# A four-layer convolution and attention sequence: the last layer's 3x3 convolution by minimal filtering, its experts mixed a stage earlier

## The chip, the cores and the metric

The kernel runs on one core of a Trainium2 chip. The metric is the device time of one execution in microseconds (us); lower is better. The core has TensorE (PE, its weight loads PEld), VectorE (DVE), ScalarE (ACT), GpSimd (POOL) and SyncE (SP, which here only issues DMAs). Each engine works through its own queue in order.

## What is computed

The input is 8 images of 512 channels, 32 x 32 pixels, fp32. Four layers follow each other. Layer 0: group norm, q, k, v, attention with 8 heads, three steps of an inner iteration, a projection. Layer 1: attention over one head with q and k of 64 channels. Layer 2: separable up- and downsampling with a leaky ReLU between. Layer 3 is the one that the change is about: a bottleneck whose weights are mixed for each image out of 8 experts.

```
pooled = x.mean(axis=(2, 3))
rw = jax.nn.sigmoid(pooled @ router_w.T + router_b)       # 8 weights per image
W = jnp.einsum('be,eoihw->boihw', rw, experts)            # for w1, w2, w3
out = relu(bn1(conv1x1(x, W1)))                           # 512 -> 128 channels
out = relu(bn2(conv3x3(out, W2)))                         # 128 -> 128
out = relu(bn3(conv1x1(out, W3)) + x)                     # 128 -> 512
```

## The kernel before, in words

`tile_sequence` handles one image after another through layers 0 to 2 (`layer0`, `layer1`, `layer2`), and puts each image's result z (2 MB) to DRAM (`spilled`). Layer 3 then runs over all 8 images. The last image's z stays in SBUF. Activations lie with channels on the partitions: `[128, 4, 1024]`, 16 KB a partition, out of one pool of seven buffers (`big_tile`). PSUM is split into `ps_sc` (two pairs of banks), `ps_tp` and `ps_mm` (two banks each).

A scheduler orders the instructions of each engine, by the order of the program among what it thinks ready, so that a later stage's work may move ahead on an engine that it takes for idle. Inside `tc.manual_schedule(engines=...)` the named engines keep the order in which the code is written: that is so for PE, DVE and ACT in layer 0's attention, and for PE in `layer2`.

What matters for the change:

- `layer0` makes q, k and v by `product`: seven products P1, C11, U2, U3, C22, C21, C12 of quarter matrices, each some TensorE work followed by a `made` step that takes PSUM away. For q and k (`channels`) ACT copies P1 before C11 goes on in the same bank and takes C11; DVE takes the rest. For v (`positions` with a row) DVE takes all. The code writes three such products after each other; an `Exp` of one element ("early") behind k loads ACT's table ahead of attention.
- Attention runs 64 steps; per step ACT takes an exponential of 128 x 1024 into one of six `tmp` buffers, and DVE adds it into a `sums` buffer (two exist), two SBUF inputs.
- The inner iteration is three `product`s with tanh on ACT and sums on DVE.
- `layer2_constants` (L133) builds the up- and downsampling operators from iotas and filter taps: 14 iotas and two broadcast loads on POOL, many small DVE instructions. It stands in image 0's layer 1, behind the value product.
- `out_of_bounds` (L1218) counts overflows and loads the verdict into a register of every engine, for a second pass that is normally skipped. In the code it stands ahead of layer 3; the register loads of PE, DVE and ACT were scheduled at the very end.
- Layer 3 before: all experts are held in SBUF, w1 in a pool of its own and three thirds of w2 and w3 in four big buffers, loaded during layer 2 of the last image. `route` makes the weights of images 0 to 6 at once, and of image 7 later. `mixed(b)` (L1204) makes an image's weights: per part one ACT multiplication and seven DVE multiply-adds. It is called one image ahead.
- One image of layer 3: c1 (L324, 2 halves of 4 matmuls of 512 columns), ReLU into a zero-rimmed plane `rim`; c2 (L1272, 9 taps for 2 halves, so 18 matmuls); ReLU into h2; c3 (L1286, 4 blocks of 2), each followed by a DVE multiply-add onto z, an ACT ReLU and an output DMA.

Each fp32 matmul of the program is two TensorE instructions in the profile.

Of the kernel before, what the change touches and what calls it, by code (L numbers as in the profile page):

```python
# [37 lines left out]
QR = C // 2  # L38
PARTS = ("A11", "A12", "-A22", "S1", "S2", "S3", "S4")
# [14 lines left out]
def tile_sequence(ctx: ExitStack, tc: tile.TileContext, a: dict, out: bass.AP, shifted: bool):  # L54
# [78 lines left out]
    def layer2_constants():  # L133

        setup, apart = tmp("setup", S), tmp("setup_apart", S)
# [7 lines left out]
        def iota(name, pattern, base, per_partition=0):  # L143
            t = scratch(name, pattern[0][1])
            nc.gpsimd.iota(
                t, pattern, base=base, channel_multiplier=per_partition,
                allow_small_or_imprecise_dtypes=True,
            )
            return t
# [15 lines left out]
        taps_up = scratch("taps_up", NTAP)  # L165
        nc.gpsimd.dma_start(taps_up, a["up_filter"].partition_broadcast(P))
        nc.vector.tensor_scalar_mul(taps_up, taps_up, 2.0)
        taps_dn = scratch("taps_dn", NTAP)
        nc.gpsimd.dma_start(taps_dn, a["down_filter"].partition_broadcast(P))

        part = iota("part", [[1, 1]], 0, 1)
        tap = iota("tap", [[1, NTAP]], 0)

        def rows_of(name, width):

            row = scratch(f"row_{name}", 1)
            first = iota(f"first_{name}", [[width, (P - 1) // width]], width)
            nc.vector.tensor_scalar(first, first, part, None, ALU.is_le)
            nc.vector.tensor_reduce(row, first, AX.X, ALU.add)
            col = scratch(f"col_{name}", 1)  # L180
            nc.vector.scalar_tensor_tensor(col, row, float(-width), part, ALU.mult, ALU.add)
            return row, col

        def tap_index(name, n, step, base, mul, by):

            t = iota(f"ix_{name}", [[step, n]], base)
            add = scratch(f"add_{name}", 1)
            nc.vector.tensor_scalar_mul(add, by, float(mul))
            nc.vector.tensor_scalar_add(t, t, add)
            return t  # L190

        def outer(op, rows, cols):
# [13 lines left out]


        in_c, in_r = rows_of("in", IR)
        ur = placed("ur", tap_index("ur", UR, -1, 17, -2, in_r), taps_up)
        outer(up_op, ur, placed("uc", tap_index("uc", UC, 1, 11, -2, in_c), taps_up))  # L210
        outer(
            up_left_op, ur, placed("ucl", tap_index("ucl", UC, 1, 11 - 2 * EDGE, -2, in_c), taps_up)
        )
        up_rr, up_cc = rows_of("up", UC)
        outer(
            dn_op,
            placed("dr", tap_index("dr", OR, 2, -6, 1, up_rr), taps_dn),
            placed("dc", tap_index("dc", OC, 2, 0, -1, up_cc), taps_dn),
        )
        in_c, in_r = rows_of("in63", 3)  # L220
        outer(
            up63_op[:, 0 : 2 * W],
            placed("ur63", tap_index("ur63", 1, 0, 10, -2, in_r), taps_up),
            placed("uc63", tap_index("uc63", 2 * W, 1, 5, -2, in_c), taps_up),
        )
        outer(
            dn63_op,
            placed("dr63", iota("dr63", [[2, 3]], 1), taps_dn),
            placed("dc63", tap_index("dc63", W, 2, 6, -1, part), taps_dn),
        )  # L230
# [18 lines left out]
    pooled = const.tile([P, CC, B], F32, name="pooled")  # L249
    spilled = [spill.tile([C, S], F32, name=f"spill_{run}_{b}", tag=f"spill_{b}") for b in range(B)]  # L250
# [338 lines left out]
    def layer0(b, x, norm, w):  # L589
# [8 lines left out]
        q = big_tile(f"q_{b}", [P, CC, S])  # L598
        k = big_tile(f"k_{b}", [P, CC, S])
        v = big_tile(f"v_{b}", [P, SC, C])  # L600
        all_of(product(f"q_{b}", w["q"], h, t, channels(f"q_{b}", q, qkv_b[:, 0:CC])))
        if b == 0:
            nc.vector.tensor_add(row_bias, row_bias, bias2)
        w["inl"] = weight("inl", b)
        all_of(product(f"k_{b}", w["k"], h, t, channels(f"k_{b}", k, qkv_b[:, CC : 2 * CC])))
        w["proj"] = weight("proj", b)
        early = small.tile([P, 1], F32, tag="early", bufs=1, name=f"early_{b}")
        tc.keep_in_program_order(nc.scalar.activation(early, eps, AF.Exp))
        all_of(product(f"v_{b}", w["v"], h, t, positions(f"v_{b}", v, v_row), rows=True))
        w["v1"] = weight("v1", b)  # L610
# [145 lines left out]

        all_of(inner)
        for it in (1, 2):
            t = quarter_sums(f"hf_{b}_{it}", hf)
            name = f"inl_{b}_{it}"  # L760
            all_of(product(name, w["inl"], hf, t, inner_step(name, hf)))
# [7 lines left out]
    def layer1(b, x, w, midway):  # L769
# [77 lines left out]
        if b == 0:  # L847
            layer2_constants()
# [249 lines left out]
    with tc.tile_pool(name=f"weights_{run}", bufs=1) as wpool:  # L1098
# [10 lines left out]
        late_loads()  # L1109

# [20 lines left out]
    WCOLS = 2 * C + 9 * P  # L1131
    experts = {}

    def load_experts(key, n, pool=None):
        if pool is None:
            t = big_tile(f"{key}e", [P, NE, n])
        else:
            t = pool.tile([P, NE, n], F32, name=f"{key}e", bufs=1)
        nc.sync.dma_start(t, a[key])
        experts[key] = t  # L1140
# [6 lines left out]

    load_experts("w1", C, pool3)

# [11 lines left out]
    router_w = pool3.tile([P, CC, NE], F32, name="router_w", bufs=1)  # L1161
    nc.gpsimd.dma_start(router_w, a["router_wT"].rearrange("(cc p) e -> p cc e", p=P))
    router_b = pool3.tile([P, NE], F32, name="router_b", bufs=1)
    nc.gpsimd.dma_start(router_b, a["router_b"].partition_broadcast(P))
    rw = const.tile([P, B, NE], F32, name="rw")

    def route(b0, b1):

        n = b1 - b0
        mean = pool3.tile([P, CC, n], F32, name=f"mean_{b0}", bufs=1)  # L1170
        nc.vector.tensor_scalar_mul(mean, pooled[:, :, b0:b1], 1.0 / S)
        ps = bank(ps_tp, f"router_{b0}")
        for cc in range(CC):
            nc.tensor.matmul(
                ps[0:n, 0:NE], mean[:, cc, :], router_w[:, cc, :],
                start=(cc == 0), stop=(cc == CC - 1),
            )

        apart = pool3.tile([n, n, NE], F32, name=f"apart_{b0}", bufs=1)
        nc.vector.tensor_tensor(  # L1180
            apart, ident[0:n, 0:n].unsqueeze(2).to_broadcast([n, n, NE]),
            ps[0:n, 0:NE].unsqueeze(1).to_broadcast([n, n, NE]), ALU.mult,
        )
        ps = bank(ps_tp, f"routed_{b0}")
        nc.tensor.matmul(
            ps[:, 0 : n * NE], ones[0:n, :], apart.rearrange("k b e -> k (b e)"),
            start=True, stop=True,
        )
        nc.vector.tensor_tensor(
            rw[:, b0:b1, :], ps[:, 0 : n * NE].rearrange("p (b e) -> p b e", e=NE),  # L1190
            router_b.unsqueeze(1).to_broadcast([P, n, NE]), ALU.add,
        )
        nc.scalar.activation(rw[:, b0:b1, :], rw[:, b0:b1, :], AF.Sigmoid)

    route(0, B - 1)


    rims = []
    for i in range(2):
        t = pool3.tile([P, H + 2, W + 2], F32, tag=f"rim_{i}", bufs=1, name=f"rim_{i}")  # L1200
        nc.gpsimd.memset(t, 0.0)
        rims.append(t)

    def mixed(b):  # L1204
        wt = pool3.tile([P, WCOLS], F32, tag="mixed", name=f"mixed_{b}")
        parts = [("w1", 0, C)]
        parts += [(f"w2_{ky}", C + ky * 3 * P, 3 * P) for ky in range(3)]
        parts += [("w3", C + 9 * P, C)]
        for key, at, n in parts:
            src, dst = experts[key], wt[:, at : at + n]  # L1210
            nc.scalar.activation(dst, src[:, 0, :], AF.Copy, scale=rw[:, b, 0:1])
            for e in range(1, NE):
                nc.vector.scalar_tensor_tensor(
                    dst, src[:, e, :], rw[:, b, e : e + 1], dst, ALU.mult, ALU.add
                )
        return wt

    def out_of_bounds():  # L1218
# [10 lines left out]
        nc.vector.tensor_add(count, count, count0)  # L1229
        ps = bank(ps_tp, "within")  # L1230
# [5 lines left out]
    z3 = {}  # L1236

    def freed(t):
        if t == 4:
            load_experts("w2_0", 3 * P)  # L1240
            z3[0] = load_z(0)
        elif t == 6:
            for ky in (1, 2):
                load_experts(f"w2_{ky}", 3 * P)
        elif t == 7:
            load_experts("w3", C)

    z_last = layer2(B - 1, halo, freed)
    z_next = z3[0]
    redo = None if shifted else out_of_bounds()  # L1250
    wt_next = mixed(0)
    route(B - 1, B)
    for b in range(B):
        z, wt = z_next, wt_next
        if b + 1 < B:
            z_next = load_z(b + 1) if b + 2 < B else z_last
            wt_next = mixed(b + 1)
        h1 = rims[b % 2]
        for g in range(2):
            ps = bank(name=f"c1_{b}_{g}")  # L1260
# [105 lines left out]
```

## Time and profile before

| | |
|---|---|
| time, median of 3 runs | 3780.77 us (3780.32 to 3782.17) |
| the profiled execution's own time | 3779.3 us |
| its span | 3777.5 us, mean granted TensorE clock 0.997 |
| instructions | 50171 |
| DMA | 248.67 MB, mean 66 GB/s over the span |

The page lists busy time by engine, the chain of work that ended last, and groups of instructions. A group's line has source line, engine, operation, output<-inputs, shapes, count, then busy us and mean ns of one, then the idle time before and what released it. A stage table has, per stretch of the span: its length, then busy us and instructions of PE, PEld, DVE, ACT and POOL, the granted clock, the share of the DMA engines and GB/s. A wait line reads: waiting engine, tile and line, what it waited for, then total us, times and longest.

The shape of the run: the start takes 14.7 us, an image 436 to 450 us up to the end of layer 2, and layer 3 the last 247.9 us.

### The profile page before, as it was taken

The numbers are of one execution on the slowest core, as the hardware profiler recorded it, in microseconds if no ns is written. First come the engines' busy times: TensorE is split into PE (matmuls) and PEld (weight loads), VectorE is DVE, ScalarE is ACT, GpSimd is POOL, SyncE is SP. The second block draws the span as 40 slices with busy tenths as digits, with TensorE's granted clock in tenths as the row PEclk, the third lists the DMA queues.
The fourth block names the chain that finished last, engine by engine and source line by source line (L and its number), as shares of the span: only waits on it lengthen the run. The fifth ranks groups of instructions, "written<-read, shape, count | busy, mean of one in ns | idle before, by whom it ended". The sixth has DMA issues, their size and how long they took to land.

```text
span 3777.5 us, 50171 instructions
## 1 busy us (share of the span) xinstructions
PE 3733.1 (99%) x20838; PEld 1985.0 (53%) x20838; DVE 2550.6 (68%) x3589; ACT 1200.6 (32%) x1716; POOL 85.2 (2%) x115
## 2 busy tenths in 40 slices
PE   8999999999999999999999999999999999998998
PEld 4346653475435753476534754367534754357543
DVE  4877548665676648765586657766487656866885
ACT  1631225212442216312352125422262133421332
POOL 4000000000000000000000000000000000001000
PEclk9999999999999999999999999999999999999999
DMA  5002310122101320013101220023201131004432
GB/s 205 21 3 85 120 59 1 52 79 96 40 1 64 120 81 1 17 70 120 59 1 62 96 88 21 1 81 105 80 1 42 65 119 40 1 1 132 157 152 94
DMA packets 86193, 248.67 MB, mean 66 GB/s; under 512 B 10480, under 2 KB 33024, under 8 KB 79168
## 3 DMA queue, kind: packets, MB, share of 16 engines
q1 hardware_dynamic: 70528, 221.67, 16.6%
q10 hardware_dynamic: 13824, 12.59, 1.0%
q0 software_dynamic: 1600, 11.07, 0.8%
q8 instruction: 166, 2.72, 0.3%
q14 instruction: 75, 0.61, 0.1%
HBM read 185.40 MB, written 59.90 MB: 65 GB/s over the span
## 4 chain that ended last, share of the span: by engine, by line
PE 96%; DVE 2%; DMA 1%; issue 0%; ACT 0%; POOL 0%; SPq 0%; ACTq 0%; DVEq 0%; POOLq 0%
PE scores L640 12%; PE av L681 12%; PE inl_X L435 7%; PE up L1019 5%; PE dn L1037 5%; PE inl_A L435 4%; PE v_X L435 4%; PE inl_Y L435 4%; PE av_X L953 4%; PE c L1272 3%; PE v_A L435 3%; PE v_Y L435 3%; PE av_Y L953 3%; PE av_A L953 3%; PE proj_X L435 2%; PE q_X L435 2%
## 5 line engine op out<-in xcount | busy, mean ns | idle before, releaser
L659 ACT ACTIVATE e<-scores 128x1024 f32<-128x1024 f32 x504 | 516.2, 1024 | 668.3 <-PE scores L640 661.4
L640 PE MATMUL scores<-q,k 64*64 64x512 f32 x4096 | 532.1, 592 | 0.0
L681 PE MATMUL av<-e,v 64*64 64x512 f32 x4096 | 528.8, 589 | 0.0
L665 DVE TENSOR_TENSOR acc<-acc,e 128x1024 f32<-128x1024 f32 x320 | 389.3, 1216 | 37.4 <-ACT e L659 35.4
L640 PEld LDWEIGHTS scores<-q,k 64*64 64x64 f32 x4096 | 150.7, 133 | 295.2 <-issue 216.8
L681 PEld LDWEIGHTS av<-e,v 64*64 64x64 f32 x4096 | 156.8, 133 | 282.7 <-issue 276.7
L435 PE MATMUL inl_X<-T_hf,w_inl 128*128 128x512 f32 x576 | 261.6, 592 | 0.0
L1003 DVE SCALAR_TENSOR_TENSOR up<-up,leak 128x512 f32<-128x512 f32 x264 | 173.8, 687 | 125.9 <-ACT leak L1002 120.9
L702 DVE RECIPROCAL inv<-av 128x256 f32<-128x256 f32 x128 | 223.0, 1747 | 2.0 <-PE av L694 2.0
L1002 ACT ACTIVATE leak<-up 128x512 f32<-128x512 f32 x264 | 149.8, 596 | 206.1 <-DVE up L1003 132.9
L1037 PEld LDWEIGHTS dn<-dn_op,up 128*64 128x64 f32 (+1 forms) x4096 | 187.9, 136 | 18.2 <-issue 18.2
L1037 PE MATMUL dn<-dn_op,up 128*64 128x99 f32 (+5 forms) x4096 | 194.0, 253 | 0.0
L1019 PE MATMUL up<-halo,up_op 126*128 126x512 f32 (+1 forms) x384 | 182.0, 601 | 9.4 <-DVE up L1003 9.4
L435 PEld LDWEIGHTS inl_X<-T_hf,w_inl 128*128 128x128 f32 x576 | 108.8, 190 | 138.4 <-issue 112.2
L435 PE MATMUL inl_A<-hf,w_inl 128*128 128x512 f32 x384 | 174.3, 597 | 0.0
L531 ACT ACTIVATE inl_U<-inl_U,inl_b 128x512 f32<-128x512 f32 x96 | 66.7, 718 | 302.7 <-DVE inl_U L546 302.7
L663 DVE TENSOR_TENSOR acc<-e,e 128x1024 f32<-128x1024 f32 x64 | 79.4, 1240 | 107.2 <-ACT e L659 92.4
L542 DVE TENSOR_TENSOR inl_U<-inl_X,inl_P 128x512 f32<-128x512 f32 x96 | 61.8, 685 | 113.9 <-PE inl_X L435 112.9
L1272 PE MATMUL c<-rim,mixed 128*128 128x512 f32 x288 | 125.5, 593 | 0.0
L1019 PEld LDWEIGHTS up<-halo,up_op 126*128 126x128 f32 (+1 forms) x384 | 72.0, 191 | 97.3 <-issue 66.3
L435 PEld LDWEIGHTS inl_A<-hf,w_inl 128*128 128x128 f32 x384 | 71.6, 190 | 97.2 <-issue 86.5
L953 PE MATMUL av_A<-v,eT 128*128 128x256 f32 x512 | 122.3, 384 | 0.0
(299 smaller groups left out, 5534.5 us busy)
## 6 DMA issues: line engine op xcount, KB each, us to landing
halo<-ypad_u SPq DMA_DIRECT2D x128, 252.0 KB
halo<-ypad_u SPq DMA_DIRECT2D x128, 198.0 KB
w_v<-stored_u_v SPq DMA_DIRECT2D x14, 1792.0 KB
x<-in_x_dram SPq DMA_DIRECT2D x32, 512.0 KB
spill_u<-z SPq DMA_DIRECT2D x28, 512.0 KB
z<-spill_u SPq DMA_DIRECT2D x28, 512.0 KB
out_dram<-z SPq DMA_DIRECT2D x28, 512.0 KB
w_q<-stored_u_q SPq DMA_DIRECT2D x7, 1792.0 KB
```

What stands on the lines that cost most here:

```text
L435: nc.tensor.matmul(dst, lhs, rhs, start=(opens and s == 0 and cc == 0), stop=(cc == 1 and s == rows), skip_group_check=True,)
L640: nc.tensor.matmul(ps[r][rows[c]], k[rows[r], oc, jc * P + c * HD : jc * P + c * HD + HD], q[rows[r], oc, ts(sh, HALF)], start=True, stop= ...
L659: nc.scalar.activation(e, pair, AF.Exp, scale=HD ** -0.5)
L665: nc.vector.tensor_add(accs[g], accs[g], e)
L681: nc.tensor.matmul(avs[g][r][rows[c]], v[rows[r], jc, ts(2 * oc + c, HD)], e[rows[r], ts(c, HALF)], start=(jc == 0), stop=(jc == SC - 1),)
L702: nc.vector.reciprocal(copies[g][:, at], totals[g][:, at])
L953: nc.tensor.matmul(ps[:, ts(s, QR)], left[:, j, at : at + P], right[:, j, :], start=(what in ("P1", "U2", "W") and s == 0 and j == 0), sto ...
L1002: nc.scalar.mul(t, ps, 0.2 * SQRT2)
L1003: nc.vector.scalar_tensor_tensor(dst, ps, SQRT2, t, ALU.mult, ALU.max)
L1019: nc.tensor.matmul(ps[i], op[0 : IR * n, :], halo.tile(t)[0 : IR * n, c + i, :], start=True, stop=True,)
L1037: nc.tensor.matmul(rows[part, r0 - first : r1 + 1 - first, c0 : c1 + 1], up[t][0:k, c, ts(2 * cc + s, HD)], op[:, r0 - 4 * t + 3 : r1 + 4 ...
L1272: nc.tensor.matmul(banks[g].rearrange("p (h w) -> p h w", w=W), wt[:, at : at + P], h1[:, ky + 16 * g : ky + 16 * g + 16, kx : kx + W], st ...
```

## The change

Four things change together.

The 3x3 convolution goes by minimal filtering along rows. Two neighbouring outputs of a row need four inputs d0..d3 and three taps g0, g1, g2. `spread` makes d1+d2, d3−d1, d2−d1, d0−d2 on DVE, `transform_weights` makes (g0+g2)/2 ± g1/2 on ACT and DVE, and `c2` multiplies four parts of three rows: 12 matmuls of 512 columns. Two parts are then combined through ACT copies and two DVE instructions. h2 comes out by even and odd columns, and c3 and its evictions follow that (`apart`, a stride of two elements in z).

The experts of image b are mixed in `layer0` of image b+1, by ACT multiplications and POOL additions (`premix`), and the mixed weights go to DRAM (`mixed`). They are read from DRAM for every image, in nine pieces of 256 columns. Layer 3 loads an image's mixed weights from there (`load_weights`). Image 7's experts are mixed inside layer 3, during images 0 to 5. `route` takes one image and broadcasts the mean over 128 columns.

In layer 3, PE, DVE and ACT keep the written order, as do ACT and SP in q, k, v of images 1 to 7. The bounds count moves behind images 5 and 6.

The operators of layer 2 are built in image 0's inner iteration, two sections per step.

```diff
-        all_of(product(f"q_{b}", w["q"], h, t, channels(f"q_{b}", q, qkv_b[:, 0:CC])))
...
+        fixed = tc.manual_schedule(engines={mybir.EngineType.Activation, mybir.EngineType.SP}) if b else nullcontext()
+        with fixed:
+            q = big_tile(f"q_{b}", [P, CC, S])
+            parts = product(f"q_{b}", w["q"], h, t, channels(f"q_{b}", q, qkv_b[:, 0:CC]))
+            for _ in range(2):
+                next(parts)
+            mixing = iter(())
+            if b:
+                mixing = premix(b - 1)
+                next(mixing)
+                route(b - 1, pooled_mean(b - 1))
+            for _ in range(2):
+                next(mixing, None)
+            all_of(parts)
...
+            w["inl"] = weight("inl", b)
+            k = big_tile(f"k_{b}", [P, CC, S])
...
+            for _ in range(2):
+                next(parts)
...
+            tc.keep_in_program_order(nc.scalar.activation(early, eps, AF.Exp))
+            for _ in range(3):
+                next(mixing, None)
+            all_of(parts)
+            w["proj"] = weight("proj", b)
+            for _ in range(2):
+                next(mixing, None)
+            v = big_tile(f"v_{b}", [P, SC, C])
...
+            next(parts)
+            all_of(mixing)
+            all_of(parts)
```

```diff
+    def premix(b, halves=False):
+        half, slots = NE // 2, 2 if halves else 3
+        read = big_tile(f"experts_{b}", [P, 2, NE, QR])
...
+        for i in range(slots):
+            load(i)
+        yield
+        for i, (at, n) in enumerate(pieces):
...
+            scaled(0)
+            scaled(1)
+            if halves:
+                yield
+            added(lo[:, 0:2, :], lo[:, 0:2, :], hi[:, 0:2, :])
+            scaled(2)
+            added(lo[:, 2, :], lo[:, 2, :], hi[:, 2, :])
+            added(lo[:, 0, :], lo[:, 0, :], lo[:, 2, :])
+            scaled(3)
+            added(lo[:, 3, :], lo[:, 3, :], hi[:, 3, :])
+            added(lo[:, 1, :], lo[:, 1, :], lo[:, 3, :])
+            added(dst, lo[:, 0, :], lo[:, 1, :])
+            if i % 2 == 1 or i == len(pieces) - 1:
...
+                nc.gpsimd.dma_start(mixed[b][:, first : at + n], acc[:, 0 : at + n - first])
+            if i + slots < len(pieces):
+                load(i + slots)
+            yield
```

Here `load` is an SP DMA of a piece (the third slot lies in the two `sums` buffers), `scaled(e)` two ACT multiplications, of experts e and e+4, and `added` a POOL addition.

```diff
+    with tc.manual_schedule(engines={engines.PE, engines.DVE, engines.Activation}):
         for g in range(2):
-            ps = bank(name=f"c1_{b}_{g}")
...
+            c1(0, g)
+        mean = pooled_mean(B - 1)
+        transform_weights(0)
+        mixing = premix(B - 1, halves=True)
+        next(mixing)
+        route(B - 1, mean)
+        spreads[0] = spread(0)
+        for b in range(B):
+            more = b + 1 < B
+            if more:
+                if b + 2 < B:
+                    zs[b + 1] = load_z(b + 1)
+                wts[b + 1] = load_weights(b + 1)
...
+            c2(b, main, 1, True, False)
+            nc.scalar.copy(one, main)
+            for _ in range(2):
+                next(mixing, None)
+            c2(b, odd, 3, True, True)
+            c2(b, main, 2, False, False)
+            nc.scalar.copy(two, main)
+            nc.vector.scalar_tensor_tensor(one, one, 2.0, two, ALU.mult, ALU.subtract)
+            nc.vector.tensor_add(one, odd, one)
             nc.scalar.activation(
...
+                h2[:, ts(1, HALF)], one, AF.Relu, bias=bn[1][1], scale=bn[1][0]
+            )
+            if more:
+                for g in range(2):
+                    c1(b + 1, g)
+                transform_weights(b + 1)
+            c2(b, main, 0, False, True)
             nc.scalar.activation(
...
+                h2[:, ts(0, HALF)], main, AF.Relu, bias=bn[1][1], scale=bn[1][0]
+            )
+            if more:
+                spreads[b + 1] = spread(b + 1)
+            next(mixing, None)
+            c3(b, h2)
...
+            if b == 5:
+                count = out_of_bounds()
+            elif b == 6:
+                redo = counted(count)
```

```diff
+    def transform_weights(b):
...
+        nc.scalar.mul(g1, g1, 0.5)
+        nc.vector.tensor_add(even, g0, g2)
+        nc.vector.scalar_tensor_tensor(even, even, 0.5, g1, ALU.mult, ALU.subtract)
+        nc.vector.scalar_tensor_tensor(g1, g1, 2.0, even, ALU.mult, ALU.add)
...
+    def spread(b):
+        d = [rim[:, :, k : k + W - 1 : 2] for k in range(4)]
...
+        nc.vector.tensor_add(to[1], d[1], d[2])
+        nc.vector.tensor_sub(to[3], d[3], d[1])
+        nc.vector.tensor_sub(to[2], d[2], d[1])
+        nc.vector.tensor_sub(to[0], d[0], d[2])
+        return t
...
+        for i in (1, 0):
+            for oc in range(2):
+                multiply(oc, i)
+                if i == 0:
+                    finish(oc)
+        for oc in (2, 3):
+            for i in (1, 0):
+                multiply(oc, i)
+            finish(oc)
```

The last block is the end of the new `c3`; `multiply` is one matmul, `finish` a block's DVE multiply-add, ACT ReLU and output DMA. `c1` and `c3` are the bodies of before as functions, with c1 in `ps_tp` banks.

```diff
+        operators = layer2_constants() if b == 0 else iter(())
+        next(operators, None)
         all_of(inner)
         for it in (1, 2):
...
-            all_of(product(name, w["inl"], hf, t, inner_step(name, hf)))
+            parts = product(name, w["inl"], hf, t, inner_step(name, hf))
+            for i, _ in enumerate(parts):
+                for _ in range(2 if i < 4 else 0):
+                    next(operators, None)
+        all_of(operators)
...
-        if b == 0:
-            layer2_constants()
```

## The prediction

> **What bounds the kernel now.** I read the page's busy times first, then the chain that ended last.
>
> ```profile
> PE 3733.1 (99%) x20838; PEld 1985.0 (53%) x20838; DVE 2550.6 (68%) x3589; ACT 1200.6 (32%) x1716; POOL 85.2 (2%) x115
> PE 96%; DVE 2%; DMA 1%; issue 0%; ACT 0%; POOL 0%; SPq 0%; ACTq 0%; DVEq 0%; POOLq 0%
> ```
>
> TensorE is both the busiest engine and the path. Time is won by giving it fewer instructions or closing its gaps (44 us); POOL is free, ACT two thirds free. Next, busy time by stage: start, image 0, image 1, image 7 up to layer 3, layer 3.
>
> ```profile
> 0.00:14.72 14.72, 1.18 (x5) 1.00 (x5) 9.14 (x30) 2.06 (x3) 5.09 (x14) 1.00 0.89 289
> 14.72:461.90 447.18, 439.73 (x2534) 236.80 (x2534) 309.75 (x468) 138.44 (x198) 45.60 (x57) 0.99 0.22 77
> 461.90:898.00 436.10, 435.85 (x2537) 234.97 (x2535) 289.95 (x398) 139.13 (x200) 3.56 (x4) 1.00 0.17 58
> ...
> 3079.50:3529.60 450.10, 439.78 (x2543) 235.25 (x2541) 298.90 (x420) 145.18 (x211) 13.14 (x20) 0.99 0.18 61
> 3529.60:3777.50 247.90, 237.31 (x558) 102.44 (x556) 193.21 (x292) 80.23 (x104) 0.00 (x0) 0.98 0.32 124
> ```
>
> An image takes 436 us with PE full; image 0 takes 11 us more, image 7 14 us more. TensorE's own waits name why:
>
> ```profile
> PE up L1019 <- DVE up L1003: 9.4, 9, 7.0
> PE xT L857 <- DVE y L858: 5.2, 1, 5.2
> ```
>
> The 5.2 us is image 0's: 58 small operator-building instructions stand on DVE from 328.8 to 354, between the evictions that PE needs. The 7.0 us is image 7's: DVE mixes experts (L1213) from 3470.8 to 3476.4 while PE waits for its leaky ReLU. Last, the TensorE timeline of one layer 3 image (start, length):
>
> ```profile
> 3590.17 7.03 PE L324 MATMUL c<-z,mixed 128*128 128x512 f32 x16
> 3597.03 15.62 PE L1272 MATMUL c<-rim,mixed 128*128 128x512 f32 x36
> 3612.49 7.31 PE L1286 MATMUL c<-h,mixed 128*128 128x512 f32 x16
> 3619.63 7.03 PE L324 MATMUL c<-z,mixed 128*128 128x512 f32 x16
> ```
>
> The 3x3 takes (3612.49 − 3597.03)/36 = 0.4294 us an instruction, two instructions to a matmul. L1286 takes 7.14 instead of 16 × 0.4294 = 6.87: its first weights wait for ACT.
>
> [...] While POOL adds at 92–98 us, DVE's sums (1.22 us otherwise) take
>
> ```profile
> L665 DVE TENSOR_TENSOR acc<-acc,e 128x1024 f32<-128x1024 f32 x3 | 5.4, 1814 | 0.3
> L367 POOL TENSOR_TENSOR w_v<-w_v,raw_v 128x512 f32<-128x512 f32 x1 | 2.3, 2262 | 0.0
> ```
>
> and POOL's add 2.26 for 1.26, whereas DVE's PSUM evictions kept 0.69 beside POOL. [...] After the 7.0 us gap four matmuls took 3.78 us, elsewhere 1.88. [...]
>
> **The change part by part** (against the span of 3777.5 us; the run that was profiled took 3779.3, 1.8 more, and the median of the runs is 1.5 above that).
>
> 1. *Convolution.* Per image 12 matmuls instead of 18: 8 × 12 instructions × 0.4294 = **−41.2**. All on the path. c3 now begins with the half that is ready long before, and 1.7 us of PE work covers the ReLU (0.78) of the other: 8 × 0.27 = **−2.2**.
>
> 2. *The work that the convolution gains.* In order on PE: c2's parts 1, 3, 2 (2.6 us each), c1 of the next image (6.9), part 0, c3; 24.05 us an image. Between c1's end (14.6) and the next image's part 1 (24.05) stand ACT's ReLU 0.77 and halving ~0.6 (384 elements, L1211's 0.60), two DVE steps of 0.61 and four sums of 544 elements (0.72 from 512 in 0.68): done at about 20.1. DVE then begins c3's eviction (1.28), whose first operand is ready at 19.8; c3's last block needs a bank from it at 22.3 and has it at 21.4. DVE per image: 1.4 + 1.8 + 2.9 + 5.4 = 11.5; ACT 9.5 plus 5 of mixing. Both lie under 24. POOL's mixing for image 7 meets the four sums and three other DVE instructions with two SBUF inputs, but POOL is busy some 7 us of an image, mostly before them. *No cost*; the cover is c2's part 0 and c3's first half. The sums' stride of two elements is in no row of this trace: bounded by 0.72 and twice that. At twice, with the evictions' stride too, c3 waits about 3 us an image (24 in all). I take the lower[...].
>
> 3. *Layer 3's start.* PE's c1 for image 0 ends at +6.9; behind it, all in fixed order, stand ReLU, halving, two DVE steps, DVE's router add, the first sum: c2 starts at about +11 less the router's matmuls: **+3.3** (0.8 if the transform is early, 5 with a cooled clock). Image 7 has no c1 between part 2 and part 0, so ACT's copy (0.58 and two semaphores) shows: **+0.9**.
>
> 4. *The register load for the bounds count* now stands in fixed PE order behind image 6's c3. It waits for a bank from DVE's evictions, for DVE's two last evictions (2.7 us) and loads (0.59 in the trace of before, where it lay at the end): **+2.9** (0 to 4).
>
> 5. *Weights from DRAM.* The next image's 1.1 MB go out when c3 of the image before frees the buffer, behind outputs and perhaps a 2.1 MB z load on one SP queue. Needed 7.7 us later. With 1 MB ahead at about 300 GB/s (the window 461–469 moved 262, the start 289 to 382), 2 us to start (1.8 MB stores landed in 6.0 to 7.7 us, some 6 of it transfer) and 0.9 for c1's part, they land at about 6.4. Lead 1.3 us, so I allow **+4** over seven images (0 to 25). Layer 3's transfers, some 46 MB in 200 us, need 230 GB/s.
>
> 6. *Image 7 before layer 3.* The mixing there vanishes from DVE, with it the 7.0 us gap, the 2 us of slow clock behind it and smaller waits: stage 450.1 to about 438: **−11.3**, old routers apart.
>
> 7. *Routing.* Eight routers of eight instructions with a 128-column weight load each. The row of that shape, L832, takes 0.85 us per eight: 6.8, less the old 1.5: **+5.3**.
>
> 8. *Mixing in q, k, v, seven times.* Nine pieces. ACT: 8 × 0.41 (interval of L1211 less a slope of 0.10 per 128) = 3.3 us, 29 in all; POOL 1.24 + 5 × 0.71 = 4.8 us, 41 in all; DMA 8.9 MB. Counting from q's start in image 1 (461.9): z's spill holds the queues to about 469 (262 GB/s in 461–469, nothing after); pieces 0 and 1, 1 MB each at some 300 GB/s, land at 473 and 476, ACT is through at 480, k's first copy is due at 488. SP's inl, proj and later x loads queue behind piece loads that wait for POOL; none is due before attention. Pieces 2 to 8 begin after k's second part (495.5, sigmoid and exp tables 1.28 each included); POOL sets the pace, since piece i+3 is loaded when POOL has added piece i: POOL starts piece 2 at 497.3, after four multiplications, and ends at 497.3 + 6 × 4.8 + 2.9 (the last piece is half as wide) = 529; piece 8 is loaded when piece 5 is added (516.5), lands at 521, and ACT ends at 523. If 256 elements cost 0.88 (0.49 fixed, as L838 has it), POOL ends at 536. The first exp is due at 535.7, the first sum, which needs the tiles of piece 8, at 537.4. *No cost*, cover 6.7 us on POOL and 12.9 on ACT. A spill of 9 us of POOL into image 0's attention cost PE nothing in the trace of before.
>
> 9. *Operators in the inner loop.* They leave layer 1 (image 0 loses 6.9 us there against image 1, and about 2.6 after it, in waits that follow): −9.6 at most. In the inner loop DVE idles 7.7 us of 24 per product and gets 8.6 and 6 us, and a taps load of 6.9 us stands ahead: up to 4 back. **−7** (−3 to −10).
>
> Sum: −41.2 − 2.2 + 3.3 + 0.9 + 2.9 + 4 − 11.3 + 5.3 − 7 = −45.3. Span 3732, run 3734, beside the median **3735**.
>
> **The rivals.**
>
> *Layer 3 is fed late.* A z load (7 us) ahead of the weights in the queue, or DVE at twice its price on strides: 24 to 28 us instead of 4. For it: all loads share a queue, and six images also read experts. Against: z buffers are free earlier, since experts no longer hold four of the big ones. 3735 − 4 + 26 = 3757.
>
> *Mixing runs into attention: slower.* Place: the `sums` buffers of piece 8, which attention's first DVE sum needs. Price: six exp buffers at 1.7 us cover about 8 us, so PE waits seven times for all that POOL ends after 546; from 552 on (45/7 = 6.4 more) the change loses. If POOL ran at 2.26 for 512 all along, a piece takes 8.6 and the end is 554: 8 × 7 = 56 lost: 3735 + 56 = 3791. Against: no DVE instruction in q, k, v has two SBUF inputs. For: 9 MB loads and a fixed ACT order in a place where PE had no wait before.
>
> *It doesn't do what it says.* Copies and transforms expose as much per image as the six matmuls take (5.2 us): only items 6 to 9 stay, −13, and strides or table loads take those: 3777.
>
> **How the numbers follow.** Forecast 67%, spanning 3717 (items 3 to 5 at their low ends, 9 at its best) to 3755; fed late 16%, to 3771; no effect 6%; slower 11%. What a measurement can tell from no change is 0.2%, 7.6 us. Faster 0.83, same 0.06, slower 0.11. The range 3717 to 3771 leaves out the last two and a few per cent below.
>
> **What would show it.** 192 instead of 288 matmuls in c2 and a layer 3 image of 24 us on PE; PE waits in layer 3 only at its start, at image 7's part 0 and after image 6; no 5.2 us `xT` wait and no 7.0 us `up` wait; q, k, v still 73 us with ACT done before the first exp. Wrong if PE waits for a weights DMA in every image, for ACT in k's first part, or for exps after v.

## The result and the profile after

| | before | after |
|---|---|---|
| time, median | 3780.87 us (3780.32 to 3782.17) | 3743.14 us (3741.14 to 3744.03) |
| span of the profiled execution | 3777.5 us | 3741.8 us |
| DMA | 248.67 MB | 328.92 MB |

The ratio is 0.9899, 95% interval 0.9882 to 0.9916: 37.7 us less, against 45 forecast. First the page's busy times and the chain that ended last, of the kernel after:

```profile
PE 3699.0 (99%) x20786; PEld 1973.2 (53%) x20786; DVE 2436.7 (65%) x3396; ACT 1429.6 (38%) x2286; POOL 441.3 (12%) x586
PE 97%; DVE 2%; DMA 0%; ACT 0%; issue 0%; SPq 0%; ACTq 0%; DVEq 0%
```

ACT and POOL took the mixing (229 and 356 us more), PE still is the path. The stage table, in the columns of before: image 0, image 1, image 7, layer 3.

```profile
14.78:454.00 439.22, 438.64 (x2535) 235.41 (x2535) 310.84 (x468) 138.44 (x198) 45.63 (x57) 1.00 0.22 79
454.00:890.94 436.94, 436.69 (x2543) 235.64 (x2543) 290.32 (x400) 169.17 (x274) 47.69 (x63) 1.00 0.24 81
...
3075.81:3516.93 441.12, 437.43 (x2538) 234.73 (x2538) 280.08 (x383) 169.88 (x278) 54.80 (x76) 1.00 0.27 90
3516.93:3741.80 224.87, 201.44 (x458) 88.16 (x458) 94.18 (x124) 104.17 (x164) 48.63 (x59) 0.96 0.47 173
```

Image 0 lost 8.0 us, image 7 9.0, layer 3 23.0; images 1 to 6 together went from 2617.6 to 2621.8, some 0.7 each. Sum −35.7, all of the difference of the spans. Of layer 3's 224.9 us PE worked 201.4, so it is there that time is missing. TensorE's waits of the kernel after:

```profile
...
PE c L414 <- DMA weights<-mixed_u: 4.6, 1, 4.6
PE c L414 <- issue: 4.4, 1, 4.4
PE c L1337 <- issue: 2.4, 1, 2.4
PE up L1137 <- DVE up L1121: 2.4, 8, 0.9
PE c L1337 <- DVE spread L1327: 2.4, 1, 2.4
...
PE up L1137 <- DVE y L1034: 1.9, 1, 1.9
```

The 5.2 us `xT` wait and the 7.0 us `up` wait are gone. New are four long waits in layer 3: twice c1 (L414) for something that only once shows its name, the weights' DMA; once c2 (L1337) for the first sum, at the start; once c2 after a register load, at image 7. Layer 3 on TensorE's timeline, from image 1's c2 to image 2's c1 (start, length, idle before and releaser in brackets):

```profile
3553.08 7.89 PE L1337 MATMUL c<-spread,weights 128*128 128x512 f32 x18
3560.80 7.03 PE L414 MATMUL c<-z,weights 128*128 128x512 f32 x16
3567.67 2.74 PE L1337 MATMUL c<-spread,weights 128*128 128x512 f32 x6
3570.24 7.03 PE L1355 MATMUL c<-h,weights 128*128 128x512 f32 x16
3577.11 7.89 PE L1337 MATMUL c<-spread,weights 128*128 128x512 f32 x18
3589.43 8.80 PE L414 MATMUL c<-z,weights 128*128 128x512 f32 x16 [4.43 <-issue]
```

Image 1 takes 3577.11 − 3553.08 = 24.03 us, every instruction back to back. In image 2 c1 starts 4.43 us late and its 16 instructions take 8.80 us for 7.03: the clock is slow behind the gap, 0.56 granted from 3589.5 to 3593.0. The same again in image 4 (4.58 and 8.80, 0.56 from 3644.1 to 3647.6). The other two long waits have a slow clock behind them as well (0.67 from 3527.3 to 3530.8, 0.53 from 3712.9 to 3716.4): 18 instructions that take 7.89 us elsewhere take 9.69 and 9.62.

```profile
3527.24 9.69 PE L1337 MATMUL c<-spread,weights 128*128 128x512 f32 x18 [2.38 <-DVE spread L1327]
...
3712.87 9.62 PE L1337 MATMUL c<-spread,weights 128*128 128x512 f32 x18 [2.42 <-issue]
```

### The profile page after: what moved, and what is told of

It reads as the page before. It is cut to its first block, busy times and chain, and to the rows that moved or that the text cites. A ratio compares the mean times of both kernels' runs of the same rounds, so it can differ in the third digit from the quotient of the medians.

```text
span 3741.8 us, 51411 instructions
## 1 busy us (share of the span) xinstructions
PE 3699.0 (99%) x20786; PEld 1973.2 (53%) x20786; DVE 2436.7 (65%) x3396; ACT 1429.6 (38%) x2286; POOL 441.3 (12%) x586
## 2 busy tenths in 40 slices
DMA packets 168582, 328.92 MB, mean 88 GB/s; under 512 B 12864, under 2 KB 112208, under 8 KB 162192
## 4 chain that ended last, share of the span: by engine, by line
PE 97%; DVE 2%; DMA 0%; ACT 0%; issue 0%; SPq 0%; ACTq 0%; DVEq 0%
PE scores L754 12%; PE av L795 12%; PE inl_X L525 6%; PE up L1137 5%; PE dn L1155 5%; PE v_X L525 5%; PE av_X L1071 4%; PE inl_Y L525 4%; PE inl_A L525 4%; PE av_Y L1071 3%; PE v_Y L525 3%; PE av_A L1071 3%; PE v_A L525 3%; PE proj_X L525 2%; PE q_X L525 2%; PE k_X L525 2%
## 5 line engine op out<-in xcount | busy, mean ns | idle before, releaser
L317 POOL TENSOR_TENSOR experts<-experts 128x256 f32<-128x256 f32 (+2 forms) x297 | 238.0, 815 | 980.2 <-ACT experts L312 645.6
L312 ACT ACTIVATE experts<-experts,rw 128x256 f32<-128x256 f32 (+1 forms) x576 | 229.5, 483 | 80.6 <-DMA experts<-in_experts_dram 75.3
L957 POOL TENSOR_TENSOR seen<-seen,acc 128x512 f32<-128x512 f32 x16 | 20.2, 1264 | 1946.9 <-DVE acc L949 1946.3
```

Of the source, the lines that this page charges most:

```text
L312: nc.scalar.activation(t[:, e, :], t[:, e, :], AF.Copy, scale=rw[:, b, which : which + 1])
L317: nc.gpsimd.tensor_add(dst, x, y)
```

## Experiments

Times are medians; each ratio is to the kernel before on the same chip, where that kernel took 3780.9 to 3782.9 us. Differences of a microsecond or two between kernels are therefore read from the traces and not from the medians.

**The late weights.** What SP issues around image 2's stall, kernel after:

```profile
3576.86 0.56 SPq L294 DMA_DIRECT2D experts<-in_experts_dram  x1
3577.52 2.63 SPq L1377 DMA_DIRECT2D out_dram<-z  x4
3580.26 2.22 SPq L1282 DMA_DIRECT2D weights<-mixed_u  x3
```

and the windows behind it (share of the DMA engines and GB/s at the end):

```profile
3577.00:3582.00 5.00, 5.00 (x13) 2.26 (x12) 1.30 (x1) 4.22 (x7) 0.00 (x0) 1.00 0.70 173
3582.00:3587.00 5.00, 3.00 (x7) 0.97 (x6) 1.19 (x2) 2.31 (x6) 4.62 (x5) 1.00 1.02 403
3587.00:3591.00 4.00, 1.57 (x3) 0.84 (x4) 0.40 (x2) 0.81 (x1) 1.28 (x2) 0.86 1.05 394
```

A load of 1 MB of experts for image 7 has stood at the queue's head since 3564.5. It waits 12.3 us until ACT (8.3) and POOL (4.0) have freed a slot, as SP's waits from 3560 to 3580 show:

```profile
SPq L294 <- ACT experts L312: 8.3, 1, 8.3
SPq L294 <- POOL mix L317: 7.1, 2, 4.0
```

Behind it pile up 2 MB of outputs, then the weights; when it goes, over 4 MB leave as one burst, at 400 GB/s, and the weights are its end. In image 1 no load holds the queue: the weights are issued at 3556.21, 3.1 us into the image's c2, as here (3.15), but the outputs ahead of them went out from 3551.5 on, as they were made. Three kernels take the causes apart. The first loads the weights an image ahead:

```diff
-        wt = pool3.tile([P, WU], F32, tag="weights", name=f"weights_{b}")
+        wt = pool3.tile([P, WU], F32, tag="weights", bufs=3, name=f"weights_{b}")
...
-                wts[b + 1] = load_weights(b + 1)
+                if b + 2 < B - 1:
+                    wts[b + 2] = load_weights(b + 2)
+                elif b == B - 2:
+                    wts[b + 1] = load_weights(b + 1)
```

> Layer 3's weights get a third buffer and are loaded one image earlier (image 7's, which are mixed last, as before). Theory A: in images 2 and 4 the weights came late because a 1 MB experts load held the SP queue until the outputs (2 MB), the experts and the weights left as one burst. The two weights stalls (4.43 and 4.58 us) and the slow clock behind each (1.77 us) vanish: 12.5 us less, 3730.6. Rival B: layer 3 moves more bytes than the DMA engines carry, so the wait turns up at another load (z, experts) or in another image: 3740 or more.

3730.32 us (ratio 0.9862, 0.9846 to 0.9879). Both stalls and the slow clock behind them are gone, and nothing took their place. Its windows show that the bytes fit into an image's time: the burst is there as before, and with a longer lead PE doesn't wait.

```profile
3580.00:3585.00 5.00, 5.00 (x13) 2.23 (x12) 0.57 (x1) 4.72 (x10) 0.82 (x1) 1.00 0.93 259
3585.00:3590.00 5.00, 5.00 (x13) 2.27 (x12) 2.21 (x3) 2.07 (x4) 4.53 (x6) 1.00 1.02 414
3590.00:3595.00 5.00, 5.00 (x13) 2.13 (x13) 0.18 (x1) 1.86 (x4) 0.56 (x1) 1.00 1.06 387
```

The second takes the outputs out of the queue, the bytes stay:

```diff
-                nc.sync.dma_start(out[b, ts(oc, P), ts(part, n)], dst)
+                nc.scalar.dma_start(out[b, ts(oc, P), ts(part, n)], dst)
```

> The outputs of layer 3 are issued by ACT instead of SP, right behind the ReLU that makes them; the bytes are the same. Theory A (the SP queue: outputs pile up behind the experts load that waits, and the weights behind the outputs): the outputs leave as they are made, the weights are issued 2.6 us earlier into emptier DMA engines, the stalls shrink from 9.0 us to 0 to 3: 3731 to 3736. Rival B (bytes): the same burst, 3742 to 3744. What it may cost on ACT: four issues an image, under 0.5 us each, beside an ACT that is half idle: nothing.

3731.49 us (0.9868, 0.9851 to 0.9884). The weights go out at 3576.48 instead of 3580.26 (0.2 us into the image's c2 instead of 3.15), ahead of three of the four outputs. With the same bytes 1.5 of the 9.0 us of stalls stay:

```profile
PE c L414 <- DMA weights<-mixed_u: 1.2, 1, 1.2
...
PE c L414 <- issue: 0.3, 1, 0.3
```

The third leaves the experts' loads out:

```diff
             if i + slots < len(pieces):
-                load(i + slots)
+                if halves:
+                    n2 = pieces[i + slots][1]
+                    views[i + slots] = [read[:, i % 2, ts(h, half), 0:n2] for h in range(2)]
+                else:
+                    load(i + slots)
```

> Image 7's mixing in layer 3 uses its first two pieces of experts again and again instead of loading seven more (7 MB less; image 7's output is then made with other weights). ACT, POOL and DVE do the same instructions. Theory A: with no experts load in the SP queue both weights stalls go: 3730.6, and no other wait comes. Rival C: the weights come late because they are read from DRAM behind 2 MB of outputs, experts or no: the stalls stay, or move to other images, 3740 or more.

3730.47 us (0.9863, 0.9847 to 0.9880), no weights wait in it. So the weights come from DRAM behind 2 MB of outputs in time. This run also moves 7 MB less, so alone it doesn't tell the queue from the bytes; the first two keep all bytes. Together they show what makes the weights late: a load that waits at the queue's head and leaves with the outputs, 3 MB ahead of the weights.

**The register load.**

```diff
+            if b == 6 and not shifted:
+                count = compared(count)
             c3(b, h2)
```

where `compared` is `counted` without its register load, which stays behind c3.

> The matmul over the bounds count and its comparison are put ahead of image 6's c3; only the register load stays behind it. Theory: of the 4.2 us at image 7's start (2.42 waiting, 1.73 of slow clock after it) most is the chain matmul, DVE comparison, register load behind the last evictions; what stays is a load of about 0.6 us: 3739.5. Rival: PE waits for the load itself (its reading and branch), then 3743 stays.

3738.60 us (0.9884, 0.9868 to 0.9901), 4.5 less. On the timeline c2 of image 7 follows c3 of image 6 at once:

```profile
3703.56 0.19 PE L1309 MATMUL within<-ones,count 128*1 128x1 f32 x2
3703.68 7.13 PE L1358 MATMUL c<-h,weights 128*128 128x512 f32 x16
3710.65 7.89 PE L1340 MATMUL c<-spread,weights 128*128 128x512 f32 x18
```

With its value ready early the load shows no gap at all; the chain matmul, comparison, load in PE's fixed order was the cost.

**The convolution alone.** The direct 3x3 in the changed kernel: two rims, no `spread`, no transform, and

```diff
+            for g, ps in enumerate((main, odd)):
+                for ky in range(3):
+                    for kx in range(3):
+                        at = C + (3 * ky + kx) * P
+                        nc.tensor.matmul(
+                            ps.rearrange("p (h w) -> p h w", w=W), wts[b][:, at : at + P],
+                            rims[b % 2][:, ky + 16 * g : ky + 16 * g + 16, kx : kx + W],
```

> Of the changed kernel only the convolution goes back: 18 matmuls an image over nine taps, two rims, outputs in order; mixing, routing, operators and the fixed order of layer 3 stay. Theory: the 48 instructions saved on PE are worth 41.2 us, and with 29 us an image the weights are no longer late (12.5 us of stalls go), nor are the start's sums (2.4 with the slow clock) and image 7's copy (0.7): 3743.1 + 41.2 - 15.6 = 3768 or so. That would put all the rest of the change at 12 to 13 us of gain against the kernel before. Rival: most of the gain is in the other parts (mixing moved, operators moved) and the saved matmuls are given back as exposed work: 3750 or less.

3767.04 us (0.9961, 0.9947 to 0.9975). An image takes 3584.54 − 3555.35 = 29.19 us on PE:

```profile
3555.35 15.62 PE L1412 MATMUL c<-rim,weights 128*128 128x512 f32 x36
...
3584.54 15.62 PE L1412 MATMUL c<-rim,weights 128*128 128x512 f32 x36
```

The 8 × 5.16 = 41.3 us come back in full; 17 of them are made up for, because the two stalls (12.5), the start's wait (4.2) and the copy's (0.7) do not exist with the longer image. The register load's gap does exist (2.47). So minimal filtering was worth 23.9 us here, and could have been worth 41; the rest of the change gives 14.

**The operators.** First back to layer 1 in the changed kernel (`all_of(layer2_constants())` after the loop over `values`), then the other way round: the kernel before gets the new builder (one big buffer, counts first, sections) in its new place.

> Only the operators of layer 2 go back to their place in layer 1 of image 0, in one block, as before. Theory: image 0 gives back the 8.0 us that it gained, the xT wait of 5.2 us returns: 3751. Rival: the new way of building them (one buffer, counts made first on GpSimd) was what helped, and the place matters little: 3743 to 3746.

3759.10 us (0.9939, 0.9922 to 0.9955): 16 more, neither theory. In its trace image 0 takes 13.9 us more than in the kernel after, the start 1.4 more. The new builder takes a big buffer, which in layer 1 comes free only behind a `v_X` matmul: POOL counts at 341.6, and DVE's building runs from 342.8 to 377.4 (before 328.8 to 354.4), into the sums of the next product, where PE waits 6.3 us:

```profile
PE av_X L1067 <- DVE av_U L1041: 6.3, 1, 6.3
```

The 16 instructions behind that wait take 6.41 us for 3.62, and waits of 1.9, 1.5 and 0.9 us stand elsewhere in the image; that is most of the 13.9. This kernel therefore doesn't price the place alone. The other direction:

> The kernel before, with the operators of layer 2 made in image 0's inner loop as in the changed kernel; nothing else. Theory: image 0's stage loses the 8.0 us that it lost in the changed kernel: ratio to before 0.9979, 3773. Rival: putting them back into the changed kernel cost 16 us because of what else changed around them, and in the kernel before the place is worth 16 too (3765), or nothing (3779 to 3781).

3772.61 us (0.9974, 0.9965 to 0.9983), 10.3 less than the kernel before on that chip (6.4 to 13.2 by the interval). In the trace image 0, up to image 1's first q, takes 438.9 us for 447.2: about the 8 us of the kernel after. So the 8 us do not hang on the other parts of the change. They belong to the new builder and its new place together; the old builder in the new place was not run.

**The cover of the mixing in q, k, v.** The last addition of each piece, once and three times more:

```diff
-            added(dst, lo[:, 0, :], lo[:, 1, :])
+            for _ in range(1 if halves else 2):
+                added(dst, lo[:, 0, :], lo[:, 1, :])
```

> In the mixing in q, k, v the last addition of each piece (128x256, 0.74 us) is done twice: 9 x 0.74 = 6.7 us more on GpSimd in each of seven images, whose end moves from q+72.4 to about q+79. Theory, the prediction's item 8 with its threshold: PE waits only for what GpSimd ends after the first exp + 10 (q+84.5): no cost, 3743 to 3745. Rival: there is no slack left since GpSimd's end is already at the first exp: 7 x 6.7 = 47, or a part of it, 3755 to 3790.

3742.97 us (0.9898, 0.9881 to 0.9914): nothing, with POOL's end 6.3 us later in image 1 than in the kernel after, counted from q. In this profile neither of layer 3's gaps of 2.4 us was followed by a slow clock, and its execution (3739.95) is the fastest of the four; the others took 3742.5 to 3743.8. The gap at the start:

```profile
3527.66 7.99 PE L1338 MATMUL c<-spread,weights 128*128 128x512 f32 x18 [2.38 <-DVE spread L1328]
```

> The same with three additions more per piece: 20 us more on GpSimd, its end at about q+92.5. Theory: 8 us beyond the threshold of q+84.5, seven times: 56 us more, 3799, with PE waiting for exps or sums early in attention. Rival D: piece 8's buffers are not what attention needs first, or GpSimd's work there is hidden as well: 3743 to 3755. In between would mean that the threshold is later than the prediction had it.

3758.94 us (0.9940, 0.9923 to 0.9956): 15.8 more, 2.3 an image, where 8 were expected. The mechanism is the one of the rival that ended slower, DVE's first sum held up by piece 8's buffers:

```profile
539.18 1.23 DVE L778 TENSOR_TENSOR acc<-e,e 128x1024 f32<-128x1024 f32 x1 [10.05 <-POOL experts L317]
540.51 6.88 DVE L780 TENSOR_TENSOR acc<-acc,e 128x1024 f32<-128x1024 f32 x5
```

and TensorE's wait for it, through ACT's exp buffers, once in each of seven images:

```profile
PE scores L755 <- ACT e L774: 8.5, 7, 1.6
```

In image 1 PE waits 1.20 us, with the first exp at 529.92 and the first sum at 539.18: by estimate it would have gone on without a wait up to a first sum at 538.0, the first exp + 8.1. What counts is when the buffer that the sum takes is free. By its releaser and its time that is one of piece 8's two buffers, the one with experts 4 to 7: POOL's last addition that reads it ended at 539.15. POOL itself ended 7 us later (546.3), with the repeated additions into `mix`. A smaller part comes through ACT: its last multiplications, which wait for the last experts load, ended at 530.0, so that the first exp came at q + 75.7 instead of q + 74.6. All of TensorE's waits for exps and sums add up to 11.4 of the 15.8 us; where the rest goes is not shown.

**All together.** Weights ahead, split count, and layer 3's start re-ordered:

```diff
+        transform_weights(0)
         for g in range(2):
             c1(0, g)
         mean = pooled_mean(B - 1)
-        transform_weights(0)
         mixing = premix(B - 1, halves=True)
         next(mixing)
-        route(B - 1, mean)
         spreads[0] = spread(0)
+        route(B - 1, mean)
...
-        ps = bank(ps_tp, name=f"c1_{b}_{g}")
+        ps = bank(name=f"c1_{b}_{g}") if b == 0 else bank(ps_tp, name=f"c1_{b}_{g}")
```

> The weights one image ahead and the split count together, and layer 3's start re-ordered: the weights' transform ahead of image 0's c1, the four sums ahead of the router's addition, c1 of image 0 in other PSUM banks than those of layer 2's last evictions. Theory: 12.8 (weights) and 4.5 (count) add up, and of the start's 0.84 + 2.38 + 1.8 of slow clock some 4 go: 3722. If the three share a cause (for instance the slow clock needs several gaps), they do not add: 3724 to 3728. If the re-ordered start only moves the wait: 3726.

3722.82 us (0.9842, 0.9828 to 0.9856), the best version: the gains add up to what was expected. At the start 0.84 us of waiting is left of 3.2, and the clock stays up:

```profile
3516.91 7.13 PE L414 MATMUL c<-z,weights 128*128 128x512 f32 x16
3523.89 0.95 PE L275 MATMUL router<-router_w,mean 128*128 128x8 f32 x8
3525.68 7.99 PE L1340 MATMUL c<-spread,weights 128*128 128x512 f32 x18 [0.84 <-DVE spread L1330]
```

## Why the prediction was right, and where not

It was right in direction and in what each part does. Of its signs one failed: PE also waits for weights, though in two images and not in every one. The time came 8 us above the forecast. One term makes up most of that; smaller errors on both sides partly cancel, which is luck.

- **Item 5, weights from DRAM: the mis-sized term.** Allowed 4, measured 4.43 + 4.58 + 2 × 1.77 = 12.5 us. The working had a lead of 1.3 us with 1 MB ahead of the weights; in images 2 and 4 it was 3 MB. It saw outputs and z loads in the queue. The experts' loads of image 7 it named only in a rival, as more traffic, and not as loads that wait at the queue's head for a slot and hold the outputs back. That is the rival "layer 3 is fed late" with another load than the one it priced and half its size. The weights ahead, the outputs elsewhere and no experts each took the stalls away.
- **Items 1 and 2, the convolution and its work:** right. 192 instructions (96 matmuls), 24.03 us an image for 24.05 worked out, the 41.3 us shown by the direct convolution. The strided sums of 544 elements took 0.71 to 0.75 us, one of the 32 took 0.98; worked out was 0.72, from 0.68 for 512 elements without a stride. That the lower of item 2's two prices would hold was the author's estimate, with no row of the trace of before behind it. The 128x1024 evictions with stride took 1.28, as those without before.
- **Items 3 and 4:** 4.2 for 3.3 at the start, of which 2.38 is waiting and 1.80 slow clock; 4.2 for 2.9 at the register load, 2.42 and 1.73. Image 7's copy 0.73 for 0.9. The waits alone were shorter than worked out. The slow clock behind them, which item 3 named as a possibility and the sum left out, made up for it, so the totals lie closer than the working deserves.
- **Item 6, image 7:** −9.0 for −11.3, its routing, old and new, about even. The mixing's gap is gone; a 1.9 us wait for layer 1's y and 0.84 for the banks of layer 2's last evictions are there instead (c1 has moved to those banks).
- **Item 7, routing:** 0.7 an image for 0.85.
- **Item 8, mixing in q, k, v:** no cost, right. The first exp came at q + 74.6, ACT's last multiplication at q + 67, POOL's end at q + 72.2; 61 and 67 were worked out for the last two, so the cover was thinner than thought. The 0.71 us for an addition of 256 elements, on which the 67 rests, was the author's estimate, with no row of that size in the trace of before; it took 0.73 to 0.74. The rival's limit for POOL's end, q + 84, was too early. As a limit for the first sum it was about right (8.1 us behind the first exp, 10.3 by its figures), but with three additions more POOL ended at q + 92.0 and that cost 2.3 us an image instead of 8, since the first sum waits for one buffer and not for POOL's end.
- **Item 9, operators:** −8.0 for −7.

The terms add up. In layer 3 item 5 came out 8.5 above, items 3 and 4 0.9 and 1.3 above and 0.2 below for the copy, and the end behind PE's last matmul, which no item had, 1.4 below (8.9 us for 10.3): 9.1. Image 7 came out 2.3 above, the routing of images 1 to 6 and the operators 1.9 below. That is 9.5 of the 9.6 us that lie between the spans' difference, −35.7, and the sum of −45.3: 13.0 above and 3.5 below.

## What to carry to other kernels

A transfer that is late is not priced by its own bytes and the bandwidth: go through its queue, and ask of each issue ahead of it what that waits for, since here an issue that waited 12.3 us also gathered into a burst of over 4 MB all that stood behind it. Where a faster stage shortens a period (29.2 to 24.0 us here), list all that was hidden by the old length; it took back 17 of 41 us. A value that the program reads back is best computed one stage before the load that reads it (4.5 us here).

## What the runs showed of the hardware

- **Behind a gap of 2.4 us the clock was slow in some executions and not in others.** At layer 3's start a wait of 2.38 us was followed by 9.69 us or more for the 18 instructions in five kernels' profiles, by 7.99 in three (outputs on ACT, no experts, one addition more). At image 7 a wait of 2.4 to 2.5 us was followed by a slow clock in five (9.62 or 9.66 for 7.89, with the direct convolution 17.39 for 15.62) and not in two (7.96; weights ahead, one addition more). So a gap of 2.4 us was followed by it in ten of fifteen cases. All ten gaps of 3.9 to 4.6 us cost 1.5 us or more (8.53 to 9.32 for 7.03), those of 0.84 us 0.1 (7.13 for 7.03). What decides after a gap of 2.4 us was not tested, nor whether the small instructions ahead of these gaps (eight of 8 columns in 0.95 us at the start) play a part. By estimate, from the two such gaps of the kernel after, which cost 9.69 − 7.89 = 1.80 and 9.62 − 7.89 = 1.73 us, two executions can differ by some 3.5 us for this alone.
- **The DMA engines moved 387 to 414 GB/s** over windows of 4 to 5 us in layer 3 (403 and 394 in the kernel after, 414 and 387 with the weights ahead), with outputs, experts and weights at once and a share of 1.02 to 1.06, where the start of the kernel before showed 382 at most, from 4 to 8 us.
